# Layer 1's in-projection of a two-layer metaformer: strips of 120 positions by 512 channels through DRAM in place of a product for each patch and 64 channels

## The chip, the cores and the metric

The kernel runs on one core of a Trainium2 chip, in fp32. The metric is device time in microseconds (us), the median of several runs. A core has five engines, each with its own instruction stream: TensorE (PE in the profile; its weight loads are PEld), VectorE (DVE), ScalarE (ACT), GpSimd (POOL) and SyncE (SP). Copies between DRAM and on-chip memory go over 16 DMA engines, which the traces here show as a ring that all queues share. SP issues most loads, POOL the indirect gathers, ACT some of the stores.

## The reference

The input x has shape 2 × 128 × 64 × 64 (images, channels, rows, columns). Four steps are added to it one after the other:

```python
x = x + L0_conv(_ln_c(x))   # four deformable convolutions (1x1, 1x1, 3x3, 7x7), fused to 128 channels
t = t + L0_ffn(_ln_t(t))    # 8 experts, top 2 of a token
x = x + L1_conv(_ln_c(x))   # below
t = t + L1_ffn(_ln_t(t))    # 64 experts, 8 tokens each
```

The change lies in the third step, and there in its first two lines:

```python
xz = jnp.einsum('ed,bdhw->behw', in_proj_w, hidden_states)           # 128 -> 512 channels
xz = lax.conv_general_dilated(xz, dwconv_w, (1, 1), [(2, 2), (2, 2)],
                              feature_group_count=2 * DI, ...)       # 5x5, each channel by itself
x, z = (xz[:, :DI], xz[:, DI:])                                      # DI = 256
...                                  # channel attention on x, position attention on z, conv1d
_, ys = lax.scan(step, jnp.zeros((b, DI, DS), x.dtype), (dA, dBu, Ct))   # 4096 steps, 16 states
...                                  # gate by silu(z), projection back to 128 channels
```

## The kernel before

**The stages.** The deformable convolution has 60 taps. For each image and each of 8 groups of 512 positions, a tap is sampled (`sample`, L712–763): POOL issues four gathers of table rows from DRAM (L705, `gather`) into a buffer v, DVE weights and adds them (L746, L748, L749), PE transposes the sum (L111, four instructions), ACT copies it to st (L753), and PE multiplies it by the tap's weights regw (L773, in `product`). So an image has 8 × 60 = 480 taps; both together have 960, and I count them through, so image 1 has taps 480 to 959. `product` also asks for the next chunk of regw (`load_chunk`, on SP's queue) four taps after the last use of the old one. Then layer 1's selective scan runs for both images, one after the other, in 2 × 8 pieces of 512 positions; a piece has 16 states × 2 halves of 128 channels, and each pair is one *unit* (512 units in all). In a unit POOL forms db from du and a broadcast row bcb (L1420), ACT the decay (L1427), DVE the scan itself (L1471) and a product (L1481), and PE adds it to the sum py (L1443). bcb is loaded by SP three loads ahead. At the end comes the expert step (`L1Ffn`, L1748 and L1757 among it; L1757 transposes activations that it reads with a step of four values, 16 B).

**Side work.** The order of the instructions on all engines is written out by hand. Work that doesn't belong to the stage is a generator (a piece of code that gives control back at each `yield`) in a queue called `rest`. `sample` takes two steps of that queue after each tap of image 1. The scan steps it by credit: each unit earns 1 and each step costs the weight that was yielded, or SMALL = 0.11 where none was (L1492–1494). `after` (L1794–1808) puts there, for each image, the end of the deformable convolution, the first expert step and then `L1Conv.convs`. So image 0's `convs` runs beside image 1's gathers, and image 1's beside the scan. In PSUM, the memory that PE writes to, it has two banks there beside the gathers and three beside the scan.

**`convs` (L1096–1189).** The normalised image is laid down in on-chip memory as `hs`: 11 strips, each of 68 rows (64 and a border of 2 above and below) and 10 columns (6 and a border of 2 left and right). A *patch* is 12 × 10 = 120 positions (KP) of a strip, which give 8 × 6 = 48 output positions (NPOS); 8 × 11 = 88 patches (NPATCH) make the image. The 5x5 convolution of one channel is then a product of the patches (120 × 88) and a *position matrix* (120 × 48) that holds the 25 weights in the right places. The position matrices lie in DRAM as `pos`, 8 blocks for 64 channels each. `position_matrices` (L1024–1045) builds them during the first image's taps 48 to 138: it fills them with zeros and writes 25 × 8 strided copies of rows of 64 weights (256 B).

For each of eight groups of 64 channels (CG), `convs` does this, between L1132 and L1186:

1. SP loads tm, the group's block of `pos`, 1440 KB, one buffer.
2. The projection: one product for each of the 88 patches (L1146), with the patch as PE's weights (128 × 120) and 64 columns of the projection weights `ipw` as the moving operand. Eight patches share a PSUM bank. A copy on ACT takes the bank to X, turned so that the patches of one channel lie side by side (L1147, run through L1108 and L1113).
3. The patch product (L1154): for each of the 64 channels the patches X[:, c, :] as weights (120 × 88) and tm[:, :, c] as the moving operand (48 columns, at a step of 64 values). Eight channels share a bank; a copy on ACT takes it to Y.
4. Transposes of Y (L1173), copies to an image buffer, and stores to `xsd` and `zsd` in DRAM (in pieces of 256 B, one row of the image). For image 1 this is done once for two groups.

After the groups come the two attentions. Copies to ACT are held back: `later` (L1104–1108) emits a copy only when two newer ones are in the list, and `last` (L1110–1115) empties the list at the end of a part. Every fp32 matmul in the code shows as two PE instructions and two weight loads in the profile.

Of the kernel before, what the change touches and what calls it, by code (L numbers as in the profile page):

```python
# [10 lines left out]
F32 = mybir.dt.float32  # L11
# [8 lines left out]
P = 128  # L20
B = 2
C = 128
H = W = 64
# [7 lines left out]
NG = NT // GT  # L31
# [133 lines left out]
def mixed(gens, n):  # L165

    todo, live = deque(gens), deque()
    while todo or live:
        if todo and len(live) < n:
            live.append(todo.popleft())  # L170
        gen = live.popleft()
        try:
            weight = next(gen)
            live.append(gen)
            yield weight
        except StopIteration:
            pass
# [832 lines left out]
NPATCH = NI * NJ  # L1010
NPOS = PH * PW
CG = 64
SMALL = 0.11
TB = 1
AHEAD = 3
BCB = 5

# [6 lines left out]
def position_matrices(env, pos):  # L1024


    nc, w = env.nc, env.d["dwconv_w"]
    n = KP * NPOS * CG
    flat = pos.rearrange("o p s c -> o p (s c)")
    for o in range(512 // CG):  # L1030
        for at in range(0, NPOS * CG, 512):
            nc.sync.dma_start(out=flat[o, :, at : at + 512], in_=env.zero[:KP, :512])
            if at % 1024:
                yield
    for t in range(25):
        dy, dx = divmod(t, 5)
        for o in range(512 // CG):
            to = bass.AP(
                pos.tensor,
                pos.offset + o * n + (dy * (PW + 4) + dx) * NPOS * CG,  # L1040
                [[((PW + 4) * NPOS + PW) * CG, PH], [(NPOS + 1) * CG, PW], [1, CG]],
            )
            src = w[t : t + 1, o * CG : (o + 1) * CG].unsqueeze(1).to_broadcast([1, PW, CG])
            nc.sync.dma_start(out=to, in_=src.to_broadcast([PH, PW, CG]))
            yield


class L1Conv:
# [5 lines left out]
    def __init__(self, env, dp, wp, x2, x3):  # L1054
        nc, d = env.nc, env.d
        self.env, self.dp, self.x2, self.x3 = env, dp, x2, x3
        self.pos = dp.tile([512 // CG, KP, NPOS, CG], F32, name="pos")
        self.wp = wp

    def constants(self):  # L1060
# [35 lines left out]
    def convs(self, b, sp, pp):  # L1096


        env, nc, d = self.env, self.env.nc, self.env.d
        bank = lambda shape, name: pp.tile(shape, F32, name=name, tag="m")  # L1100
        held = deque()

        def later(*todo):

            held.append(todo)
            if len(held) > 2:
                for f in held.popleft():
                    f()  # L1108

        def last():  # L1110
            while held:
                for f in held.popleft():
                    f()  # L1113
                yield 0.3
            yield

        copy = lambda out, in_: functools.partial(nc.scalar.copy, out, in_)

        ipw = sp.tile([P, 512], F32, name="ipw", bufs=1)
        nc.sync.dma_start(out=ipw, in_=d["in_proj_w"])  # L1120

        hs = sp.tile([P, NJ, H + 4, PW + 4], F32, name="hs", bufs=1)
        for j in range(NJ):
            nc.vector.memset(hs[:, j, :, :], 0.0)
            if j % 4 == 3:
                yield
        yield
        yield from mixed([self.norm(b, g, hs, sp, bank) for g in range(NG)], 2)

        yg = CG if b == 0 else 2 * CG  # L1130
        zst = sp.tile([NPATCH, 2, 256 // yg, NPOS], F32, name="zst", bufs=1)
        for o in range(512 // CG):  # L1132
            ch = o * CG % yg
            if ch == 0:
                Y = sp.tile([NPATCH, NPOS, yg], F32, name="Y", bufs=1)

            tm = sp.tile([KP, NPOS, CG], F32, name="tm", bufs=TB)
            nc.sync.dma_start(out=tm, in_=self.pos[o])
            X = sp.tile([KP, CG, NPATCH], F32, name="X", bufs=1)
            own = ipw[:, o * CG : (o + 1) * CG]  # L1140
            for p0 in range(0, NPATCH, 8):
                ps = bank([KP, 8, CG], "ps1")
                for k in range(8):
                    i, j = divmod(p0 + k, NJ)
                    patch = hs[:, j, PH * i : PH * i + PH + 4, :].rearrange("p y x -> p (y x)")
                    nc.tensor.matmul(ps[:, k, :], patch, own, start=True, stop=True)  # L1146
                later(copy(X[:, :, p0 : p0 + 8], ps.rearrange("p k c -> p c k")))  # L1147
                yield 0.65
            yield from last()

            for c0 in range(0, CG, 8):
                ps = bank([NPATCH, 8, NPOS], "ps2")
                for c in range(8):
                    nc.tensor.matmul(  # L1154
                        ps[:, c, :], X[:, c0 + c, :], tm[:, :, c0 + c], start=True, stop=True
                    )
                later(copy(Y[:, :, ch + c0 : ch + c0 + 8], ps.rearrange("p c s -> p s c")))
                yield 0.45
            yield from last()
            if ch + CG < yg:  # L1160
                continue

            x_half = o < 4
            for py in range(PH):
                img = sp.tile([yg, NI, W], F32, name="img", tag="io", bufs=3)
                at = (o + 1) * CG % 256 or 256
                ch = slice(at - yg, at)
                dst = self.xsd[b][ch, 3:] if x_half else self.zsd[b][ch, :]
                dst = dst.rearrange("c (i y x) -> c y i x", y=PH, x=W)[:, py, :, :]
                for x0, nx in ((0, 4), (4, 2)):  # L1170
                    ps = bank([yg, nx, NPATCH], "ps3")
                    for x in range(nx):
                        nc.tensor.transpose(ps[:, x, :], Y[:, py * PW + x0 + x, :], env.ident[:NPATCH, :NPATCH])  # L1173
                    nj = NJ if x0 + nx <= W - PW * (NJ - 1) else NJ - 1
                    to = view(img, x0, [(W, NI), (PW, nj), (1, nx)])
                    todo = [copy(to, ps.rearrange("p x (i j) -> p i j x", j=NJ)[:, :, 0:nj, :])]
                    if x0:
                        todo.append(functools.partial(nc.sync.dma_start, out=dst, in_=img))
                    later(*todo)
                    if x0 or b == B - 1:  # L1180
                        yield 0.45
            yield from last()
            if not x_half:
                nc.vector.tensor_reduce(zst[:, 0, (o - 4) * CG // yg, :], Y, AX.X, ALU.add)
                yield
                nc.vector.tensor_reduce(zst[:, 1, (o - 4) * CG // yg, :], Y, AX.X, ALU.max)  # L1186
            yield

        yield from mixed([self.position_attention(b, zst, sp, bank), self.channel_attention(b, sp, bank)], 2)
# [709 lines left out]
```

## Time and profile before

| what | value |
|---|---|
| median of 3 runs | 7880.1 us (7872.57 to 7891.26) |
| the profiled execution's own time | 7901.31 us |
| its span, first to last instruction | 7898.7 us |
| TensorE clock granted in it, mean | 0.806 of full speed |
| gathers of both images (L705), until about | 5735 us |
| of these, beside image 0's `convs` groups | 4249 to 5190 us |
| scan, until about | 7648 us |
| of this, beside image 1's `convs` groups | 6353 to 6857 us |
| last expert step | 7648 to 7898 us |
| data moved over the span | 1596.67 MB in 645198 packets, mean 202 GB/s |
| PE by stage: 4200 to 5200, 5200 to 5735 us | busy 786.28 of 1000, 295.97 of 535 us |
| DVE by stage: 4200 to 5200, 6865 to 7648 us | busy 727.23 of 1000, 697.43 of 783 us |

The profile is of one execution. A line such as "L705 POOL DMA_INDIRECT v<-table,idx x3840 | 4070.0, 1060 | ..." is a group of instructions of one line of the code: engine, operation, output and inputs by the program's names, count, then busy time in us and the mean duration of one in ns, then the engine's idle time just before them and what ended most of it. Rows with forty digits give the busy share of an engine in 40 equal slices of the span, in tenths. A table of stretches gives, for each stretch of time, its length, the busy time and instruction count of each engine, the granted clock, the share of time in which the 16 DMA engines were busy, and GB/s. A line of waits names the waiting engine with its output and line, an arrow, the engine and line that released it, then the total in us, the number of times and the longest. [...]

### The profile page before, as it was taken

What the parts mean: (1) busy time and instruction counts of PE and PEld (TensorE: products, weight loads), DVE (VectorE), ACT (ScalarE), POOL (GpSimd) and SP (SyncE); (2) the same over time, 40 slices, a digit from 0 to 9 for tenths busy, and PEclk for the clock granted to TensorE, in tenths of its full rate; (3) what the DMA queues carried; (4) which work ended last, traced back from release to release, by engine and by line L of the source; (5) the groups of instructions that cost most, each with busy time, mean ns of one, the idle gap of its engine ahead of it and who ended that gap; (6) DMA issues with size and microseconds to landing.
All of it is one profiled execution on the core that took longest, in us unless ns stands there. A gap on an engine that the chain in (4) does not pass through costs nothing. (4 is left out here: it accounts for less than half of the span.)

```text
span 7898.7 us, 67414 instructions
## 1 busy us (share of the span) xinstructions
PE 5390.6 (68%) x21313; PEld 3209.2 (41%) x21313; DVE 6077.1 (77%) x6780; ACT 1992.0 (25%) x3838; POOL 5031.9 (64%) x4589
## 2 busy tenths in 40 slices
PE   4667777667776757656666878865565679756668
PEld 3344444444444424324334555532233456412124
DVE  5878878888887887788898667787756665789992
ACT  1211111111111113211111222211163255455540
POOL 4777777777777777777777666676743334357640
PEclk8888788888788878878878778877886788877789
DMA  7887767777676778877777777777754344434444
GB/s 223 261 267 214 224 207 223 214 219 219 210 221 208 224 228 270 265 255 234 240 237 217 217 218 218 228 224 222 206 172 141 107 114 113 114 131 146 146 137 149
DMA packets 645198, 1596.67 MB, mean 202 GB/s; under 512 B 168020, under 2 KB 253180, under 8 KB 640876
## 3 DMA queue, kind: packets, MB, share of 16 engines
q0 software_dynamic: 307200, 1006.88, 42.5%
q1 hardware_dynamic: 306156, 537.52, 21.4%
q10 hardware_dynamic: 31488, 47.97, 1.7%
q8 instruction: 171, 2.80, 0.1%
q14 instruction: 183, 1.50, 0.1%
HBM read 1478.65 MB, written 115.83 MB: 202 GB/s over the span
## 5 line engine op out<-in xcount | busy, mean ns | idle before, releaser
L705 POOL DMA_INDIRECT v<-table,idx x3840 | 4070.0, 1060 | 1628.2 <-issue 1033.8
L746 DVE TENSOR_TENSOR v<-v,pw 128x2048 f32<-128x2048 f32 x960 | 2192.0, 2283 | 665.7 <-DMA v<-table,idx 466.9
L773 PE MATMUL out<-st,regw 128*128 128x512 f32 x3840 | 2270.7, 719 | 187.6 <-issue 118.6
L753 ACT COPY st<-pst 128x512 f32<-128x512 f32 x960 | 557.7, 585 | 4227.9 <-remote 1887.3
L111 PE MATMUL pst<-ident,v 128*128 128x128 f32 x3840 | 730.7, 318 | 1133.6 <-issue 962.4
L748 DVE TENSOR_TENSOR v<-v 128x1024 f32<-128x1024 f32 x960 | 1177.2, 1226 | 34.6 <-remote 1.6
L1420 POOL TENSOR_TENSOR db<-du,bcb 128x512 f32<-128x512 f32 x512 | 656.8, 1288 | 845.3 <-DVE da L1471 698.8
L773 PEld LDWEIGHTS out<-st,regw 128*128 128x128 f32 x3840 | 807.2, 233 | 864.6 <-issue 779.9
L111 PEld LDWEIGHTS pst<-ident,v 128*128 128x128 f32 x3840 | 522.4, 164 | 1512.3 <-issue 1284.6
L1443 PE MATMUL py<-sc,ident 128*128 128x512 f32 x1024 | 660.7, 752 | 230.7 <-DVE sc L1481 230.3
L1471 DVE TENSOR_TENSOR_SCAN da<-da,state,db 128x512 f32<-128x512 f32 x512 | 657.1, 1283 | 183.2 <-ACT da L1427 137.6
L749 DVE TENSOR_TENSOR v<-v 128x512 f32<-128x512 f32 x960 | 664.4, 692 | 33.0
L402 PE MATMUL po<-wa,win 128*128 128x147 f32 x2112 | 381.7, 303 | 118.1 <-issue 110.8
L402 PEld LDWEIGHTS po<-wa,win 128*128 128x128 f32 x2112 | 334.3, 201 | 228.7 <-issue 228.6
L1443 PEld LDWEIGHTS py<-sc,ident 128*128 128x128 f32 x1024 | 200.4, 229 | 529.9 <-DVE sc L1481 438.0
L1146 PEld LDWEIGHTS ps<-ipw,hs 128*120 128x120 f32 x2816 | 356.0, 207 | 121.7 <-ACT X L1108 56.4
L1146 PE MATMUL ps<-ipw,hs 128*120 128x64 f32 x2816 | 355.1, 290 | 55.2 <-ACT X L1108 40.5
L1481 DVE TENSOR_TENSOR sc<-da,bcb 128x512 f32<-128x512 f32 x512 | 354.2, 692 | 43.0 <-PE py L1443 0.5
L1427 ACT ACTIVATE da<-delta,w_A_log 128x512 f32<-128x512 f32 x512 | 354.0, 692 | 18.7 <-DVE delta L1383 2.8
L1154 PE MATMUL ps<-tm,X 120*88 120x48 f32 x2048 | 216.1, 280 | 52.1 <-ACT Y L1108 35.5
L1154 PEld LDWEIGHTS ps<-tm,X 120*88 120x88 f32 x2048 | 211.0, 187 | 98.7 <-ACT Y L1108 47.4
L402 PEld LDWEIGHTS po<-wb,win 128*128 128x128 f32 x960 | 164.2, 210 | 117.2 <-issue 117.1
(296 smaller groups left out, 4704.3 us busy)
## 6 DMA issues: line engine op xcount, KB each, us to landing
bcb<-bc SPq DMA_DIRECT2D x256, 512.0 KB
regw<-in_regw SPq DMA_DIRECT2D x192, 640.0 KB
v<-table,idx POOLq DMA_INDIRECT x3840
yd<-ys ACTq DMA_DIRECT2D x128, 256.0 KB
yc<-yd SPq DMA_DIRECT2D x32, 1024.0 KB
gb<-gd SPq DMA_DIRECT2D x16, 2048.0 KB
wt<-in_weight SPq DMA_DIRECT2D x32, 1024.0 KB
tm<-pos SPq DMA_DIRECT2D x16, 1440.0 KB
```

The lines of the kernel that those rows point to most:

```text
L111: nc.tensor.transpose(ps[:, j, :], s, ident)
L402: m()
L705: self.env.nc.gpsimd.indirect_dma_start(out=v[:, j, :], out_offset=None, in_=self.table[b], in_offset=bass.IndirectOffsetOnAxis(ap=idx[:, ...
L746: nc.vector.tensor_tensor(v4, v4, w, ALU.mult)
L748: nc.vector.tensor_tensor(up, up, v4[:, :, 2:4, :], ALU.add)
L749: nc.vector.tensor_tensor(v4[:, :, 0, :], v4[:, :, 0, :], v4[:, :, 1, :], ALU.add)
L753: nc.scalar.copy(st, pt.rearrange("p j t -> p (j t)"))
L773: nc.tensor.matmul(self.out[half], self.regw[t // CH][:, t % CH, half * P : (half + 1) * P], st, start=first, stop=last,)
L1146: nc.tensor.matmul(ps[:, k, :], patch, own, start=True, stop=True)
L1420: nc.gpsimd.tensor_tensor(dbs[u], pieces[k]["du"][:, half, :], bcb[u // 2][:, 0, :], ALU.mult)
L1443: nc.tensor.matmul(py[k, half], by, what, start=first, stop=last)
L1471: nc.vector.tensor_tensor_scan(s, s, dbs.pop(u), state[:, half, n : n + 1], ALU.mult, ALU.add)
```

## The change

The projection no longer runs for each patch and group. It runs once for an image, in *strips*: 120 consecutive positions of a strip of `hs` (12 rows of 10) as weights and all 512 channels of `ipw` as the moving operand. A strip column of 680 positions takes five such products and one of 80 positions, so an image has 66. ACT copies each result to xz (three buffers) and then stores it to DRAM from its own queue, in runs of 512 values (2 KB). Within a strip the rows that two patches share are computed once and read twice; the columns that two strips share are still computed twice.

`columns(o, j)` reads patches back on SP's queue: for 64 channels o and strip j the eight patches of that strip, 960 pieces of 64 values (256 B). X has two buffers now, its layout is patches outside and channels inside, so X[:, :, c], PE's weights in the patch product, has a step of 64 values between its columns. The 11 loads of a group are issued together in the first step of the group before it (those of the first two groups while the strips end and while the first tm arrive).

The position matrices are in 16 blocks for 32 channels (TG) with three buffers, loaded two blocks ahead; their building writes 400 copies of rows of 32 weights (128 B). For image 0 the copies held back are emitted down to one before the patch product takes its next bank (`room`), and a step holds four channels' products instead of eight (`yield` in the middle). `ipw`, `hs` and xz lie in a pool `ca` that is closed before `cb` with tm and Y opens. The transposes, stores and attentions are as before.

```diff
+TG = 32
+SR = PH + 4
...
-    n = KP * NPOS * CG
+    n = KP * NPOS * TG
...
-    for o in range(512 // CG):
-        for at in range(0, NPOS * CG, 512):
+    for o in range(512 // TG):
+        for at in range(0, NPOS * TG, 512):
             nc.sync.dma_start(out=flat[o, :, at : at + 512], in_=env.zero[:KP, :512])
-            if at % 1024:
-                yield
+        yield
     for t in range(25):
...
-            nc.sync.dma_start(out=to, in_=src.to_broadcast([PH, PW, CG]))
-            yield
+            nc.sync.dma_start(out=to, in_=src.to_broadcast([PH, PW, TG]))
+            if o % 2:
+                yield
...
+        self.strips = [dp.tile([NJ, (H + 4) * (PW + 4), 512], F32, name=f"xz{b}", tag=f"xz{b}") for b in range(B)]
...
+        def room():
+            while len(held) > 1 and b == 0:
+                for f in held.popleft():
+                    f()
+
+        strip, X = self.strips[b], {}
+
+        def columns(o, j):
+
+            if j == 0:
+                X[o] = sp.tile([KP, NPATCH, CG], F32, name="X", bufs=2)
+            src = bass.AP(
+                strip.tensor,
+                strip.offset + j * (H + 4) * (PW + 4) * 512 + o * CG,
+                [[512, KP], [PH * (PW + 4) * 512, NI], [1, CG]],
+            )
+            nc.sync.dma_start(out=X[o].rearrange("p (i j) c -> p i j c", j=NJ)[:, :, j, :], in_=src)
...
+            for j in range(NJ):
+                for a, y in enumerate(range(0, H + 4, SR)):
+                    n = min(SR, H + 4 - y) * (PW + 4)
+                    ps = bank([KP, 512], "ps1")
+                    own = hs[:, j, y : min(y + SR, H + 4), :].rearrange("p y x -> p (y x)")
+                    nc.tensor.matmul(ps[:n, :], own, ipw, start=True, stop=True)
+                    xz = ap.tile([KP, 512], F32, name="xz", bufs=3)
+                    to = strip[j, y * (PW + 4) : y * (PW + 4) + n, :]
+                    later(copy(xz[:n, :], ps[:n, :]), functools.partial(nc.scalar.dma_start, out=to, in_=xz[:n, :]))
+                    if a == 5 and j:
+                        columns(0, j - 1)
+                    yield 0.4
+            yield from last()
+        with self.env.tc.tile_pool(name=f"cb{b}", bufs=1) as yp:
+            yield from self.patches(b, sp, yp, bank, room, later, last, copy, columns, X)
+
+    def patches(self, b, sp, yp, bank, room, later, last, copy, columns, X):
...
+        def matrices(q):
+            if q < 512 // TG:
+                tm[q] = yp.tile([KP, NPOS, TG], F32, name="tm", bufs=3)
+                nc.sync.dma_start(out=tm[q], in_=self.pos[q])
...
+        columns(0, NJ - 1)
+        yield 0.4
         for j in range(NJ):
+            columns(1, j)
             if j % 4 == 3:
+                yield 0.4
+        yield 0.4
...
         for o in range(512 // CG):
...
-            tm = sp.tile([KP, NPOS, CG], F32, name="tm", bufs=TB)
-            nc.sync.dma_start(out=tm, in_=self.pos[o])
-            X = sp.tile([KP, CG, NPATCH], F32, name="X", bufs=1)
-            own = ipw[:, o * CG : (o + 1) * CG]
-            for p0 in range(0, NPATCH, 8):
-                ps = bank([KP, 8, CG], "ps1")
-                for k in range(8):
-                    i, j = divmod(p0 + k, NJ)
-                    patch = hs[:, j, PH * i : PH * i + PH + 4, :].rearrange("p y x -> p (y x)")
-                    nc.tensor.matmul(ps[:, k, :], patch, own, start=True, stop=True)
-                later(copy(X[:, :, p0 : p0 + 8], ps.rearrange("p k c -> p c k")))
-                yield 0.65
-            yield from last()
...
             for c0 in range(0, CG, 8):
+                room()
                 ps = bank([NPATCH, 8, NPOS], "ps2")
+                q = (o * CG + c0) // TG
                 for c in range(8):
+                    if c == 4 and b == 0:
+                        yield
                     nc.tensor.matmul(
-                        ps[:, c, :], X[:, c0 + c, :], tm[:, :, c0 + c], start=True, stop=True
+                        ps[:, c, :], X[o][:, :, c0 + c], tm[q][:, :, c0 % TG + c], start=True, stop=True
                     )
                 later(copy(Y[:, :, ch + c0 : ch + c0 + 8], ps.rearrange("p c s -> p s c")))
+                if c0 % TG == 0 and q:
+                    matrices(q + 2)
+                if c0 == 0 and o and o + 1 < 512 // CG:
+                    for j in range(NJ):
+                        columns(o + 1, j)
                 yield 0.45
```

## The prediction

> **What bounds the kernel now.** I read the page first, then the table of busy time by stretches of 200 us, then the timeline of PE with the waits inside the stretches that the change touches, then the DMA tables of single stretches.
>
> ```profile
> span 7898.7 us, 67414 instructions
> PE 5390.6 (68%) x21313; PEld 3209.2 (41%) x21313; DVE 6077.1 (77%) x6780; ACT 1992.0 (25%) x3838; POOL 5031.9 (64%) x4589
> ...
> DMA  7887767777676778877777777777754344434444
> ...
> L705 POOL DMA_INDIRECT v<-table,idx x3840 | 4070.0, 1060 | 1628.2 <-issue 1033.8
> ...
> L1146 PEld LDWEIGHTS ps<-ipw,hs 128*120 128x120 f32 x2816 | 356.0, 207 | 121.7 <-ACT X L1108 56.4
> L1146 PE MATMUL ps<-ipw,hs 128*120 128x64 f32 x2816 | 355.1, 290 | 55.2 <-ACT X L1108 40.5
> ...
> L1154 PE MATMUL ps<-tm,X 120*88 120x48 f32 x2048 | 216.1, 280 | 52.1 <-ACT Y L1108 35.5
> ```
>
> No engine fills the span, so there are stages. Up to 5735 us POOL issues four gathers a tap; afterwards DVE's scan sets the pace. The projection (L1146) and the patch product (L1154) run twice: for image 0 beside the gathers of image 1 (4249 to 5190 us), for image 1 beside the scan (6353 to 6857 us). The same view kept to the gather line gives the pace of a tap:
>
> ```profile
> 2000.00:2200.00 200.00, 144.68 (x141) 0.80 0.71 214
> 4603.80:4653.60 49.80, 32.14 (x31) 0.79 0.88 239
> 4653.60:4726.30 72.70, 50.30 (x49) 0.74 0.75 213
> ```
>
> The columns are the stretch, its length, POOL's busy time and gathers, granted clock, DMA share, GB/s. Row one is the gather alone: 140 gathers in 200 us are 5.71 us a tap, and POOL has hardly a gap; that is the floor. Row two is one projection stretch (L1146), row three the product and transposes behind it. Over all eight groups the projection stretches hold 236 gathers in 390.8 us (**6.62 us a tap**), the others 371 in 550.6 us (**5.94**). In the projection stretches PE is busy 336.4 of 390.8 us. So there PE is the bound, partly by waiting:
>
> ```profile
> DVE v L746 <- DMA v<-table,idx: 215.6, 83, 11.0
> ...
> PEld ps L1146 <- ACT X L1108: 54.7, 22, 6.5
> PEld ps L1154 <- ACT Y L1108: 46.9, 14, 8.2
> ```
>
> These are waits inside 4200 to 5200 us (total, times, longest): PE stands for a PSUM bank that ACT has not emptied, v buffers come free late, and DVE waits for gathers issued late.
>
> In the scan, columns as above but for all engines:
>
> ```profile
> 6320.00:6865.00 545.00, 460.86 (x3030) 347.27 (x3030) 354.07 (x407) 286.70 (x595) 233.33 (x184) 0.86 0.44 118
> 7010.00:7600.00 590.00, 384.47 (x688) 123.82 (x688) 554.14 (x562) 313.04 (x608) 405.45 (x321) 0.77 0.43 144
> ```
>
> Beside the convolution PE is busy 85% and there are 134 scan units in 545 us; without it DVE is busy 94% and 238 units take 590 us (2.48 us a unit).
>
> **The change in the gather stage.** I count the yields of the generators: two are taken a tap. Before, one group of 64 channels has 11+3 for the projection, 11 for the product, 12 for the rest: 300 in all, 150 taps. After, 69 for the strips, 6 for the handover, 252 for the groups: 327, 164 taps. The queue of side work is empty at tap 914 before and would be at 928 after, of 960, so nothing spills over.
>
> Today the 150 taps take 941 us, and 14 more at the pace that follows (276 gathers in 5200:5600, 5.80 us) 81 us: **1022 us** for the same 164 taps.
>
> PE loses 1408 pairs (170 us of busy time in the eight stretches) and gains 66 strips of two 512-column passes. A pass costs 0.53 us here (L773: 125.3 us for 236), so 70 us, in 36 taps: 1.95 us a tap, beside L773 and L111's 2.8: 4.8 of 5.71. PE is then no bound. The product spreads from 4 taps to 8, and its PSUM copies are released before the next bank is taken, so L1154's waits on ACT should go. ACT gains 66 issues (0.33 us each, as for padc) and has 75% free. At the floor: 164 × 5.71 = 936 us.
>
> What is late next is the DMA ring. Its rows:
>
> ```profile
> DMA packets 10827, 11.30 MB, mean 141 GB/s; under 512 B 8559, under 2 KB 8559, under 8 KB 10615
> ...
> q1 hardware_dynamic: 10822, 11.23, 53.3%
> ```
>
> This is 6720:6800. In 6530:6590, without small packets, 5.21 MB take 29.9% of 16 engines' 60 us: 55 us of one engine per MB. Here 53.3% of 16 × 80 is 682 us; the large bytes (9.04 MB) explain 497, so 8559 image writes of 256 B cost 185 us, **22 ns each**; three neighbouring stretches give 16 to 29. The new reads of patch columns are 88 loads of 960 pieces of 256 B, 84480 an image, a form the trace has no row for. Below: 256 B at 55 us per MB, 14 ns. Above: a read of 1 KB, from the fusion's loads in 3000:3300 (14336 packets in 628 us), 44 ns. I take 25, near the write of the same size. Engine time over 16: reads 132 us, strip writes (15.3 MB) 53, tm 40, images 51; the 164 taps need 0.71 × 5.71 = 4.05 each, 664. Sum 940 us, as long as POOL's floor. The gather held 5.7 us a tap at a share of 0.82 (210 gathers in 3000:3300) and its packets took a tenth less time there, so I neither take the floor nor a full stop: I take today's pace outside the projection, 5.94 × 164 = 974 us. **Gather stage: −48 us.**
>
> [...]
>
> Queued behind the waits: the 11 column loads of a group stand in SP's queue (0.5 us each to issue) before regw. With a third of the ring free a burst of 16.5 us drains in some 48 us; a regw chunk is asked for 6 taps (36 us) before its use. Each of 7 bursts can make one chunk up to 12 us late, 84 us at worst; six v buffers let POOL run on about three taps meanwhile, so I take 0. Three xz buffers give a strip write 1.5 taps to land: 0. The weight matrices' 200 more small writes (128 B, taps 48 to 138) fall into a stage at share 0.72: 0, at 22 ns 13 us over 16 engines at worst.
>
> **In the scan.** Yields are paid by weight. The strip phase takes 29 units where eight projections took 64, and side work ends at unit 199, not 232. The eight L1146 stretches last 213 us. After: strips 69 us of PE, scan products 29 × 1.3 (L1443, 176.3 us for 134) = 38, over PE's 0.85: 126; the 34 units that fall out run later at 2.48: 84. Sum 210: **−3 us**, for what leaves PE comes under DVE's floor. The ring has 67 units in 291 us: seven bursts of 16.5, tm 40, images 51, bcb and the rest 1.08 a unit, 279 us. It fits barely, and bcb stands behind each burst; three loads ahead are 25 us. I add 10 us for columns late at short groups. **Scan: +7.**
>
> X is now the weight operand at a step of 256 B. L1757 loads weights at 16 B steps: four take 0.63 us, contiguous ones 0.60, so +7 us an image; from the other side, 48 columns at a 256 B step take at most 90 ns a pair, 1.9 ns each, which for 88 weights makes 75 ns more, 77 us on the scan's PE. I take 0.
>
> [...]
>
> **Sum.** −48 +7 = −41 on the profiled execution's 7901.3 us (span 7898.7): 7860, −0.5%; on the median of 7880.1: **7840 us**.
>
> **Rivals.**
> 1. All transfers are hidden. For it: 0.82 of the ring did no harm. Floor 936, −86, and −3: 7791 us.
> 2. The strip phase waits like the projection did, one bank behind ACT, since only the product's banks are released early: 38 × 6.62 + 126 × 5.94 = 1000, −22; scan +10: 7868, no change.
> 3. **Slower: the 256 B read.** At p ns the ring needs 808 + 5.28p us in the gather stage and 163 + 4.62p in the scan's 291. The gain is gone from p = 34. At 44: 1040 and 366 us, +18 and +82: 7980. Against: writes at 22.
> That the change does not do what it says I exclude: the emitted order has 66 strips and 88 column loads an image.
>
> **Chances.** Forecast 0.48 (7800 to 7862), rival 1 0.10, rival 2 0.15, rival 3 0.27 (7898 to 8080). Measurement here tells about 0.2% (16 us). Faster 0.58, same 0.15, slower 0.27. The low end, 7775, holds the 14 ns bound; the high end, 7980, is the 44 ns bound. Some 0.15 lies outside.
>
> **What will show it.** Gathers per 200 us near 4200 to 5200: 135 or more (now 127 to 132). DMA share there about 0.9. Small packets per engine time: 25 ns or not. PE waiting on X or regw by DMA, or POOL's db on bcb for over 120 us, would mean rival 3. In the scan the convolution should end near unit 199 at about the same time. If the patch product's weight loads (L1203 in the changed kernel) take much over 165 ns, the stride was wrong.

## The result: slower by 1.4%

The changed kernel takes 7992.8 us (median of 4 runs, 7980.5 to 8009.0), the kernel before 7884.1 beside it: a ratio of **1.0141** (95% interval 1.0114 to 1.0167), some 109 us. The forecast was 7840, with a range of 7775 to 7980. The profiled execution of the changed kernel took 8009.0 us, its span is 8007.2 against 7898.7.

The gathers' own pace is not the same in all groups of runs (a group is a few kernels run one after the other, with the kernel before among them): 5.75 us a tap without side work in the two profiles compared here, about 5.48 in others, which I call quick, on one and the same chip too. So every run below stands by its ratio to the kernel before *in its own group*. The changed kernel itself was run again in a quick group: 1.0243.

First the page of the changed kernel: the lines of the engines, the DMA row in forty slices, the gathers, and the patch product, now L1202.

```profile
span 8007.2 us, 62920 instructions
PE 5406.0 (68%) x18761; PEld 3084.0 (39%) x18761; DVE 6077.7 (76%) x6780; ACT 1982.5 (25%) x3794; POOL 5071.2 (63%) x4589
...
DMA  7887767777677677777778999877553379334444
...
L705 POOL DMA_INDIRECT v<-table,idx x3840 | 4110.1, 1070 | 1592.8 <-issue 1045.2
...
L1202 PEld LDWEIGHTS ps<-tm,X 120*88 120x88 f32 x2048 | 362.4, 261 | 195.4 <-issue 122.1
...
L1202 PE MATMUL ps<-tm,X 120*88 120x48 f32 x2048 | 360.7, 355 | 111.8 <-ACT Y L1124 40.3
```

and the product's weight loads on the page of before, where it is L1154:

```profile
L1154 PEld LDWEIGHTS ps<-tm,X 120*88 120x88 f32 x2048 | 211.0, 187 | 98.7 <-ACT Y L1108 47.4
```

2552 PE instructions are gone, and PE is no less busy (5406 us against 5390.6). The reason stands in the lines of the product: it has the same 2048 instructions as before, but each takes 355 ns and not 280, each weight load 261 and not 187. The DMA row shows the rest: two humps, of 8 and 9 where image 0's convolution runs, and a 7 and a 9 in the scan, where all slices had 3 or 4.

Where is the time lost? The last gather starts at 5737 us and before at 5734: no loss there, and no gain. The scan, from the first to the last start of DVE's scan instruction, takes **1953** us and before **1856**: 97 of the 109 us. Six more lie between the two stages and four behind the scan. This view gives the stages of the changed kernel: strips and groups of image 0, then of image 1 (stretch, length, busy time of PE, PEld, DVE, ACT, POOL, granted clock, DMA share, GB/s):

```profile
4267.00:4467.00 200.00, 149.64 (x397) 64.86 (x396) 145.69 (x110) 58.82 (x105) 142.27 (x138) 0.90 0.90 297
4499.00:5267.00 768.00, 557.00 (x2395) 380.44 (x2396) 553.12 (x401) 144.53 (x330) 514.23 (x491) 0.80 0.92 245
6368.00:6507.00 139.00, 100.51 (x218) 37.69 (x216) 75.40 (x76) 78.54 (x144) 53.34 (x43) 0.89 0.72 210
6507.00:6871.00 364.00, 318.28 (x1405) 237.07 (x1406) 161.90 (x153) 133.04 (x296) 112.16 (x90) 0.60 0.78 158
```

and the same of before, projection and all, in the scan:

```profile
6377.00:6856.00 479.00, 421.79 (x2805) 319.16 (x2804) 297.78 (x289) 250.85 (x522) 212.28 (x168) 0.87 0.44 117
```

Read the last row of the first table against this one. In the groups PE is busy 318 of 364 us, at a granted clock of **0.60**; before it was 0.87. PE is still the engine that fills these stretches.

To see which work it is, I sorted the scan's time, record by record of the trace, by the kind of convolution work that PE had started last, and counted the scan units that begin in each. A unit without side work takes 2.45 us in all of them. "Second profile" is another execution of the same kernel, reported with the experiments.

| scan | projection or strips | product | transposes |
|---|---|---|---|
| before | 237 us, 65 units, clock 0.96 | **169 us, 37 units, clock 0.82** | 97 us, 26 units |
| before, second profile | 238 us, 65 units, 0.94 | 168 us, 37 units, 0.84 | 99 us, 26 units |
| changed | 140 us, 31 units, 0.89 | **269 us, 37 units, clock 0.54** | 94 us, 26 units |
| changed, second profile | 143 us, 31 units, 0.88 | 276 us, 37 units, 0.54 | 100 us, 26 units |

The strips do what the forecast said: 140 us, and the 34 units that fall out run later at 2.45 (83 us), 223 in place of 237. The transposes are unchanged. **The loss is the product**: for the same 37 units and the same 512 products it takes 100 us more. (The strips' gain and some 14 us spread over the rest of the scan nearly cancel.)

### The profile page after: what moved, and what is told of

Read it like the earlier page. It is cut to its first block, busy times and chain, and to the rows that moved or that the text cites. A ratio compares the mean times of both kernels' runs of the same rounds, so it can differ in the third digit from the quotient of the medians.

```text
span 8007.2 us, 62920 instructions
## 1 busy us (share of the span) xinstructions
PE 5406.0 (68%) x18761; PEld 3084.0 (39%) x18761; DVE 6077.7 (76%) x6780; ACT 1982.5 (25%) x3794; POOL 5071.2 (63%) x4589
## 5 line engine op out<-in xcount | busy, mean ns | idle before, releaser
L1496 PE MATMUL py<-sc,ident 128*128 128x512 f32 x1024 | 699.6, 792 | 246.0 <-DVE sc L1534 245.6
L1202 PEld LDWEIGHTS ps<-tm,X 120*88 120x88 f32 x2048 | 362.4, 261 | 195.4 <-issue 122.1
L1202 PE MATMUL ps<-tm,X 120*88 120x48 f32 x2048 | 360.7, 355 | 111.8 <-ACT Y L1124 40.3
L402 PE MATMUL po<-wb,win 128*128 128x147 f32 x960 | 188.4, 311 | 34.7 <-issue 33.0
L402 PE MATMUL po<-wc,win 128*128 128x174 f32 (+1 forms) x800 | 170.1, 339 | 60.7 <-issue 37.0
```

The lines of the kernel that those rows point to most:

```text
L402: m()
L1202: nc.tensor.matmul(ps[:, c, :], X[o][:, :, c0 + c], tm[q][:, :, c0 % TG + c], start=True, stop=True)
L1496: nc.tensor.matmul(py[k, half], by, what, start=first, stop=last)
```

## The experiments

Three causes could make the product slow. *A*: its patches come late, or the bursts of column loads hold up what stands behind them on SP's queue and the ring. This is how such a burst looks on SP (start, length, line, count), beside the gathers and in the scan. These two come just ahead of the groups and have twelve loads, the last of the first group and the eleven of the second; the bursts of eleven inside the groups hold the queue for 35 to 48 us and for 17 to 24.

```profile
4480.57 42.39 SPq L1137 DMA_DIRECT2D X<-xz  x12
4523.07 1.92 SPq L280 DMA_DIRECT2D regw<-in_regw  x1
```

```profile
6494.11 23.46 SPq L1137 DMA_DIRECT2D X<-xz  x12
6517.68 2.58 SPq L1488 DMA_DIRECT2D bcb<-bc  x1
```

and the waits of 6507 to 6871 us name the victim first: POOL's db for bcb, 178.7 us, against 85.4 in all groups of before.

```profile
POOL db L1473 <- DMA bcb<-bc: 178.7, 20, 23.1
ACT Y L1110 <- PE ps L1202: 138.5, 40, 15.7
DVE da L1524 <- ACT da L1480: 118.2, 24, 14.3
...
DVE da L1524 <- POOL db L1473: 20.7, 2, 13.7
```

*B*: the weights' step of 256 B in X. For it speaks the second line: ACT waits for PE, and the decay waits behind that copy on ACT. *C*: the clock, which is at 0.60 in these groups and was at 0.87: the same instructions may just run slower.

### Each suspect alone

**Neighbouring weights.** `X[o][:, :, c0 + c]` became `X[o].rearrange("p a c -> p (a c)")[:, (c0 + c) * NPATCH : (c0 + c + 1) * NPATCH]`.

> The patch product reads 88 neighbouring values of X as its weights, and not 88 values at a step of 256 B; the values are those of other patches and channels, so the output is not the reference's. All loads stay. Theory A (the bursts): the 11 column loads of a group hold SP's queue (17 to 23 us a burst in the scan, 42 us beside the gathers), bcb and regw stand behind them, and the stride costs nothing on the path: 7975 to 8000 us, POOL still waits some 180 us for bcb between the strips' end and the convolution's end in the scan. Theory B (the stride): an instruction of the product falls from 359 to about 263 ns as before the change, PE has 75 us less to do in the scan's groups, and the time falls by as much, to about 7920 us, with the granted clock there back above 0.8.

Measured: 1.0183 (1.0160 to 1.0205), and the unaltered change in a quick group, its control below, 1.0243: some 45 us less. The scan's product stretches: 243 us, clock 0.61. B is a cause, but worth 45 of the 75 us that it claimed, and the clock did not come back.

**Large pieces.** The source of a column load became `[[512, KP], [1, 512]]`, its target `X[o]` in runs of 512.

> Each column load reads 120 runs of 2 KB in place of 960 pieces of 256 B: the same number of loads and bytes, an eighth of the pieces; it reads other rows of the strips, so the output is not the reference's. Theory A: a burst holds SP's queue for about 11 times 0.5 us, POOL's wait for bcb in the scan goes back to the 85 us of before or less, the ring's share beside the gathers falls from 0.95 to about 0.8, and the time falls by 80 to 150 us, to 7840 to 7910. Theory B: the stride stays, PE is as busy as before, at most 30 us are gained: 7960 to 7990.

Measured: 1.0156 (1.0132 to 1.0180), some 65 us less than the control; 52 of them lie beside the gathers (image 0's stretches take 901 us for 160 taps, the control's 953), only 11 in the scan's product (265 us). So the pieces of 256 B cost something beside the gathers and almost nothing in the scan, where A had put the loss.

**Both.**

> Both edits together; the output is not the reference's. It shows what the strips give without the small pieces and without the stride. If A and B are separate costs their gains add up. By A alone it stands with the run of large pieces, by B alone with the run of neighbouring weights. My forecast of before for a ring without harm was 7791 us; I expect 7780 to 7850.

Measured: 1.0074 (1.0053 to 1.0095). The gains add up (1.7% against 0.6 + 0.9), but the product stretches still take 224 us.

**The bursts spread.**

```diff
-                if c0 == 0 and o and o + 1 < 512 // CG:
-                    for j in range(NJ):
+                if o and o + 1 < 512 // CG:
+                    for j in range(c0 // 4, min(c0 // 4 + 2, NJ)):
                         columns(o + 1, j)
```

> The column loads of the next group are issued two in each step of the group, and not 11 in its first step; nothing else changes. Theory A, if the burst is what hurts: bcb and regw pass between the loads, 50 to 100 us less in the scan, 7890 to 7940 us. If it is the sum of the ring's work, not its bunching, or if theory B holds: 7975 to 8000 us.

Measured: 1.0229 (1.0194 to 1.0264), the change's own 1.0243 within the interval; product stretches 283 us. POOL's waits for bcb in the whole profile are as long as with the bursts (237 us against 249). The edit parts the loads only in part: in the scan bcb loads now pass between runs of one to ten column loads, where eleven stood together. So it does not by itself clear the bunching; what does is the run without reads below, in which 25 us is all that the scan's product gains when the bursts inside the groups are gone. The longest line of the waits was not the main cause. POOL works three units ahead: of its 20 waits for bcb in that window, 18 ended with db ready 1.2 us or more before DVE's scan began, and DVE waited for db 20.7 us in all, the last line of the view.

### The control, the clock, the packing, the repair

**The changed kernel again**, as the control of the quick groups.

> [...] If the change costs the same everywhere: 1.4% over the kernel before on the same chip, a scan of about 1953 us from first to last (1856 before the change). If the loss grows where the gathers are quicker, because the ring is then fuller: 1.8 to 2.3%, as the run of spread loads, which differed little from it in its parts.

Measured: 1.0243 (1.0218 to 1.0268), scan 1966 us. The loss is larger in this quick group.

**Dense work.** For image 1, ahead of each eight products:

```diff
+                if b:
+                    nc.tensor.matmul(ps.rearrange("p c s -> p (c s)"), env.ident[:KP, :NPATCH],
+                                     X[o].rearrange("p a c -> p (a c)")[:, 0 : 8 * NPOS], start=True, stop=True)
```

> For image 1, each step of eight patch products is preceded by one dense product (128 x 88 weights, 384 columns) into the same bank, which the real ones then overwrite: 64 more products, 128 instructions, that nobody needs; the output stays the reference's. Theory C (the clock): in the patch products the array is little used, the granted clock sits at half (0.59 over the groups), and with it the scan's own py products take 0.85 us and not 0.61. Dense work raises the clock above 0.8, py falls by 0.25 us or more an instruction, and in spite of 21 us more work at full clock the scan is 20 to 60 us shorter than the control's. If the clock is only a symptom (PE is idle because it waits for loads): the clock stays near 0.6 and the scan is 20 to 45 us longer. By the theory of the bursts: no change beyond the added 20 to 40.

Measured: 1.0270 (1.0247 to 1.0293), scan 2001 us, 35 longer. The clock over the product stretches rose from 0.54 to 0.73 and py fell from 0.91 to 0.76 us (start to the next start), but a product instruction stayed at 163 ns (168). With the stride the clock does not matter to the product. C as I had put it fell.

**One step of the product a unit.** `yield 0.45` became `yield 0.45 if b == 0 else 1.0`.

> For image 1, a step of eight patch products costs a credit of 1.0 and not 0.45, so that a unit of the scan gets one step and not 2.2; the products take 64 units and not 29, the same work in the same order. If PE is the bound of these units (2.2 steps x 16 instructions x 172 ns and 1.9 us for py, some 8 us a unit): a unit then needs 4.7 us, 64 x 4.7 = 300 against 232 for 29 and 87 for the other 35 at 2.48, a gain of about 20 us. If the ring is (seven bursts in 370 us): the bursts have twice the time, bcb no longer waits, gain 50 to 90 us. If the loss is elsewhere: no change.

Measured: 1.0145 (1.0128 to 1.0162): 73 us less than the control, the largest gain of any edit that keeps the computation. The product stretches take 309 us for 71 units; the control's 276 for 37 and 34 units at 2.45 make 359. PE is busy 296 of these 309 us. The size, 50 us in these stretches and 64 in the scan, lies where I had put the ring's theory; the records of PE decide between the two. Of the 50, 36 come from PE's own work (34 further units add 47 us to it, and would have taken 83 later), 14 from idle time (27 to 13 us). I had taken py at 1.9 us a unit, and it took 1.6.

**Neighbouring weights by a copy on ACT**, in tiles of four channels:

```diff
+        def pack(i):
+            if i < 128:
+                pk[i] = yp.tile([KP, 4, NPATCH], F32, name="pk", bufs=3 if b else 6)
+                at = i % 16 * 4
+                nc.scalar.copy(pk[i], X[i // 16][:, :, at : at + 4].rearrange("p a c -> p c a"))
...
-                        ps[:, c, :], X[o][:, :, c0 + c], tm[q][:, :, c0 % TG + c], start=True, stop=True
+                        ps[:, c, :], own[:, c % 4, :], tm[q][:, :, c0 % TG + c], start=True, stop=True
```

> ACT copies X, four channels at a time (120 x 352 values, 128 copies an image), into small buffers in which the 88 patches of a channel lie side by side, and the patch product takes its weights from there; all loads stay, the output is the reference's. Theory B (the stride): as the run with neighbouring weights, the product at 0.09 (full clock) to 0.15 us, the scan 20 to 30 us shorter than the control's, less what 128 copies of some 0.5 us cost on ACT, on which the decay stands in the same queue (up to 60 us): between -30 and +30 us. It would gain more only if PE at full clock is what was missing.

Measured: 1.0237 (1.0219 to 1.0254), scan 1967 us: nothing in sum. The product's own work fell from 172 to 145 us, but PE's idle time in its stretches rose from 27 to 50. ACT's copies wait for the patches (114 us) with the decay behind them, and DVE's wait for the decay rises from 229 to 288 us.

### The kernel before, and two halves

**The kernel before again.**

> The kernel before, profiled on the chip of this group, to set its stages beside those of the other runs: if the gathers are quicker here (5.45 us a tap without side work, and not 5.75), the stretch of image 0's convolution should show what the floor no longer hides: the projection at 6.4 us a tap or more as in the first profile, if PE is the bound there. The scan should take the same 1856 us from first to last.

Measured: 7923.1 us, its group had 5.75 us a tap. The stretches are those of the first profile (second row of the table; the scan takes 1874 us, 18 more). But the run of the smaller half below has the code of before for image 1, and there the same product stretches take 151 us, at a clock of 0.92. So the product took 150 to 170 us before, by its clock, and the 169 that I compare with are the dear end.

**Large pieces, neighbouring weights and dense work.**

> The run with large pieces and neighbouring weights, and the dense products of the clock experiment added for image 1; the output is not the reference's, since the weights are other values. The scan of that run without dense work takes 1915 us, 58 more than before the change, at a granted clock of 0.66 over the groups. Theory C (without the projection between them the products let the clock fall, and here, unlike with the stride, they would be faster at full clock, 0.09 and not 0.15 us): clock above 0.8, scan 20 to 40 us shorter, ratio to before 1.002 to 1.005. If the clock is only a symptom: scan 20 to 40 us longer, 1.010 to 1.013.

Measured: 1.0048 (1.0031 to 1.0065) in a group with the slower gathers, so its ratio can't be set beside that of the run without dense work; the scans can: 1912 against 1915 us. Here the clock does what C said: 0.63 to 0.80 over the product stretches. The view of the product's instructions (least, median, most, in ns) shows it, without and with dense work:

```profile
L1202 PE MATMUL ps<-tm,X x1024: 247/339/383, 6208.8 to 6516.1; 120*88 120x48 f32 x171
```

```profile
L1210 PE MATMUL ps<-tm,X x1024: 242/263/350, 6470.1 to 6781.3; 120*88 120x48 f32 x171
```

and the changed kernel in its scan:

```profile
L1202 PE MATMUL ps<-tm,X x1024: 273/361/396, 6507.2 to 6851.0; 120*88 120x48 f32 x171
```

and the kernel before in its own:

```profile
L1154 PE MATMUL ps<-tm,X x1024: 247/262/382, 6377.6 to 6838.1; 120*88 120x48 f32 x171
```

Neighbouring weights have two speeds, one for each clock, and strided ones are slow always. The records say so without any average: where two product instructions follow each other within one state of the granted clock, the time from start to start has the median 85 ns at full clock and 147 at half with neighbouring weights, in the kernel before and in these runs alike, and 170 at both with the step. (That also clears tm, whose columns have a step of 128 B now and had 256 B: at the same clock nothing changes, 85 and 147 ns with both.) The dense work itself takes 51 us (the 21 at full clock that I had put for it in the first clock experiment were my estimate, which no run shows); the 35 us that product and py gain, and 12 us less of waiting, pay for it and no more.

**The change's smaller half** put into the kernel before: `room()` ahead of the product's bank, and for image 0 a `yield` in the middle of its eight products.

> The kernel before, with the change's smaller part alone: for image 0 the copies held back are emitted down to one before the patch product takes its bank, and a step holds four channels' products. The projection for each patch stays. If the product's waits on ACT (46.9 us in the first profile) were worth their length: 10 to 30 us faster than before, ratio 0.996 to 0.999. If the gathers set the pace there anyway: no change, within 0.2%. If the smaller steps cost: slower; I don't expect it, the queue then ends at tap 946 of 960.

Measured: 0.9994 (0.9981 to 1.0007). No difference. (Its scan, with image 1 as before, is the one with the product at 151 us.)

**The projection of before spread thinner**: the same `yield` in the middle of eight of eleven projection steps (and not in the product), `room()` ahead of both banks, and `yield 0.65 if b == 0 else 0.8`.

> The kernel before with its projection spread thinner, and not replaced: for image 0 eight of eleven projection steps of a group hold four patches and not eight, and the copies held back are emitted down to one before a bank is taken; for image 1 a projection step costs a credit of 0.8 and not 0.65, so that its eight groups take 13 units more. If PE's work per tap and per unit is what makes the projection late (6.62 us a tap with 336 of 391 us busy; 3.3 us a unit): 20 to 40 us less beside the gathers and 10 to 20 in the scan, ratio 0.992 to 0.997, and so faster than both kernels. If not: no change.

Measured: 0.9985 (0.9969 to 1.0002). Just not told from no change.

### What the reading itself costs

`columns` returns for o > 1 with `X[o] = X[o - 2]`: 66 of 88 loads are left out, with the stride and with neighbouring weights.

> The changed kernel without 66 of the 88 column loads an image: groups two to seven use the patches of groups none and one again, so the output is not the reference's; the strips are still computed and stored, and the stride stays. If the reading holds the product's stretches: beside the gathers they fall to the floor of the day (5.5 to 5.75 us a tap), and in the scan from 276 to about 220 us for 37 units, which leaves the stride's 33 and little else over the 168 of before. If the packing does: 5.9 to 6.2 us a tap and 250 us or more as before. Ratio to before: 1.005 by the first, 1.015 or more by the second.

> The same without the reads, and the product's weights are neighbouring values, as in the run before that tried this alone; the output is not the reference's. If stride and reading together are the cause: the product's stretches in the scan take 170 to 185 us for 37 units at a clock near 0.8, the scan some 1860 us, ratio to before 0.995 to 1.000. If the packing is a cause of its own: 200 us or more remain, ratio 1.004 or more.

Measured: 1.0107 (1.0086 to 1.0127) and 1.0056 (1.0037 to 1.0075). Beside the gathers 885 and 896 us for 160 taps (5.53 and 5.60), close to that group's 5.47 without side work: there the reads are nearly all that stood above the floor (953 us in the control). In the scan's product 251 and 215 us. So reading costs 25 us there, and 47 of the 107 remain without stride and reads; the run expected 170 to 185.

The records of PE inside the product stretches say what they are. "Each" is the time to the next start, or to its own end:

| product stretches of the scan | all | product, each | py, each | PE idle | clock |
|---|---|---|---|---|---|
| before | 169 us | 98 us, 96 ns | 50 us, 583 ns | 7 us | 0.82 |
| changed, second profile | 276 | 172, 168 | 64, 911 | 27 | 0.54 |
| no reads | 251 | 171, 167 | 64, 911 | 3 | 0.54 |
| neighbouring weights | 243 | 131, 128 | 55, 785 | 47 | 0.61 |
| no reads, neighbouring weights | 215 | 129, 126 | 55, 783 | 21 | 0.62 |
| large pieces, neighbouring, dense | 225 | 103, 100 (and 51 for the dense) | 42, 600 | 19 | 0.80 |

PE's own work fills all but 3 to 47 us of every row. The stride costs 42 us on the product (172 to 129) and some 9 on py, the clock some 35 more on product and py (129 + 55 to 98 + 50), the reads about 25 as idle time. The parts are taken in this order; with the stride in place the clock costs the product nothing. That the clock sets the speed of neighbouring weights is shown by the dense run and by the records. That the projection kept the product's clock up was not tried by itself, but the kernel before shows the course (product from 6424 to 6448, a projection in the last row; PE busy 10.00 in all):

```profile
6420.00:6430.00 10.00, 10.00 (x69) 6.27 (x69) 5.73 (x6) 5.08 (x11) 4.81 (x5) 1.00 0.39 122
6430.00:6440.00 10.00, 10.00 (x55) 7.00 (x54) 3.98 (x5) 4.86 (x8) 1.97 (x2) 0.57 0.11 43
6440.00:6450.00 10.00, 10.00 (x50) 7.23 (x50) 3.15 (x4) 5.11 (x12) 1.27 (x1) 0.58 0.00 1
...
6540.00:6550.00 10.00, 10.00 (x75) 8.34 (x75) 6.69 (x7) 7.64 (x12) 9.03 (x8) 1.00 0.51 190
```

This product starts at full clock behind a projection and falls to half within some 10 us; beside the projections the clock is 0.96 in the mean. The changed kernel's four product stretches, of 59 to 79 us each, have no projection between them.

### A version that beats both

PE's work per unit is what fills the convolution's units, and thinning it out (one product step a unit) brought more than any removal that kept the computation. So I took the kernel before, with image 0 as in the run with the thinner projection, and for image 1 0.75 for a projection step and 0.6 for a product step (0.65 and 0.45 before).

> The kernel before with projection and product spread thinner: for image 0 as in the run with the thinner projection; for image 1 a projection step costs a credit of 0.75 and a product step 0.6, where they cost 0.65 and 0.45, so that side work ends some 19 units later, close to unit 251 of 252. If PE's work per unit bounds the convolution: each further unit brings 1.2 us (2.45 for a unit without side work less some 1.2 for its py), 20 to 25 us in the scan and 10 to 15 beside the gathers, ratio 0.994 to 0.997. If the gaps do, or if what is left at unit 252 has to be drained: 0.998 or more.

Measured: **0.9969** (0.9953 to 0.9985), faster than both. Its scan takes 1822 us, its product stretches 141 us for 41 units, at a clock of 0.94. How much of that is the spreading and how much the clock no run separates.

## Why the prediction was wrong

The forecast was −41 us and the result +109. Of these 150 us 90 lie in the scan (+97 against +7) and 37 in the gather stage (−11 against −48); the rest are small terms.

**What failed: "I take 0" for X as the weight operand at a step of 256 B.** The bound worked out there from tm's 48 columns (1.9 ns for each value at that step, 77 us on the scan's PE) was right almost to the microsecond: the product's PE time went from 98 to 172 us, and 168 ns for 88 weights are 1.9 ns each. (A part is luck: at the clock that the change left, neighbouring weights would have taken 129.) I took the other end because L1757's weights at a step of 16 B cost nearly nothing (four in 0.63 to 0.70 us, contiguous ones 0.60). That row was the nearer one by operand and the farther one by step; step should have counted. This case shows the price at 256 B (170 ns against 85 at full clock) and little of it at 16 B. The prediction's last sign, weight loads much over 165 ns, came: their median in the scan is 263 (the line is L1202, not L1203).

**"What leaves PE comes under DVE's floor"** held for the strips (−14 us; −3 forecast), and this is also why they bring so little: 65 units at 3.65 us became 31 at 4.50 and 34 at 2.45. But the sum held the product's 37 units at their old pace, and there PE, not DVE, was already the bound before: busy 162 of 169 us. What is added to PE there is added to the time.

**The clock was not in the sum at all.** I priced the scan's PE instructions from rows taken at 0.86. With the projection gone the product's stretches run at 0.54, and what is left is dearer: py from 583 to 911 ns.

**"Columns late" +10**: 25 in the scan. Rival 3 put a price of 44 ns on a read of 256 B; by the records of the DMA engines a packet of 256 B, reads and image writes together, took 24.9 ns in 6507:6871 and 22.3 in 4499:5267. The 25 ns were right (the image writes alone, put at 22, took 18.3 before). Rival 3 had the direction, and not the mechanism. Its sign came even so: POOL waited 178.7 us for bcb, over the 120 that were named, and the runs show that this wait was worth little. A sign that a second cause can set off proves neither.

**Gather stage, −48 us: it became −11** (taps 711 to 928 in 1314 us against 1325). The price was right, the mean was wrong: I spread the reads over all 164 taps, and 78 of the 88 loads fall into the last 126. There they and the gathers ask for nearly all that the ring has, and the share is 0.92, for 768 us together. Without the reads the taps run close to the floor (5.53 us against 5.47 without side work in that group). Why the loss is larger in a quick group stays open: over the same taps the changed kernel gained 56 us there (1314 to 1258), as much as its gathers' pace gives (217 taps at 0.27 us), and the kernel before was not profiled in such a group.

**What held.** No spill-over; 138 gathers in 200 us beside the strips, where 135 or more were asked (beside the groups it is 128, 491 in 768 us); regw late by 15 us in all, as "I take 0" had it, though the loads held SP's queue longer than the 0.5 us each that I gave them (1.4 us at the median); the side work of the scan ends at unit 199 or 200. The matrices' 200 more writes, taken at 0, cost about 10 us (taps 49 to 138 at 5.97 against 5.88 us and 5.84), under the 13 given as the worst.

## What to carry to other kernels

An operand's layout is part of an instruction's price (here 170 ns for a pair of load and product at a step of 256 B and 85 with neighbouring weights, both at full clock): before a product gets another layout, find a row with *that step on that operand*, and where there is none, keep the dear end in the forecast. Work that is taken from an engine brings only what it took above the next bound (here 14 of 237 us in the scan), and if it was dense, it may have paid for the clock of its neighbours (here 0.82 in the product's stretches with the projections between them and 0.54 without). And put a load on a shared ring into the stretch in which it is issued, not into the mean over the stage (here 78 of 88 loads in 126 of 164 taps, at a DMA share of 0.92).

## What the runs showed of the hardware

- 88 weights at a step of 256 B: 170 ns for a pair of load and product, at full and at half clock (163 in the mean with the clock at 0.73). Neighbouring: 85 ns at full clock, 147 at half. At a step of 16 B there is little of it (four pairs of 128 weights in 0.63 to 0.70 us against 0.60).
- The granted clock fell to half though PE's records leave no gap. Two stretches of 10 us of the changed kernel, columns as before (PE busy 10.00 of 10.00, clock 0.50):

```profile
6540.00:6550.00 10.00, 10.00 (x53) 8.90 (x52) 2.38 (x3) 2.19 (x5) 1.34 (x2) 0.50 1.17 175
6550.00:6560.00 10.00, 10.00 (x53) 8.90 (x52) 2.95 (x4) 2.18 (x5) 0.00 (x0) 0.50 1.07 201
```

  Busy by the records was not enough to hold the clock (the ends of PE's records are modelled, so a busy PE may hold gaps that they do not show), and one dense product to sixteen instructions raised it from 0.54 to 0.73 over the product stretches.
- Eleven loads of 960 pieces issued together held SP's queue for 17 to 24 us in the scan and 35 to 48 beside the gathers; at the median a column load took 3.17 us there beside the gathers and 1.34 in the scan (1.39 over all 176), a bcb load 0.34.
- The pace of the same gathers changed between groups of runs, about 5.48 or 5.75 us a tap, on one chip too. Why, no run shows.
